# A four-layer image kernel on one core: convolutions whose operands alternate between a sample and a quarter image per 32 partitions, evictions on 128 partitions, and frames normalised once

## The chip, the cores and the metric

The kernel runs on one core of one Trainium2 chip. The metric is the device time of one execution in microseconds (us); lower is better. A run is quoted as the median of several executions. The engines are named as the profile names them: PE (matrix multiply, with PEld for its weight loads), DVE (vector), ACT (scalar and activation), POOL (GpSimd) and SP (the queue that issues most DMAs).

## The reference

The input `x` has 16 samples, 32 channels and 128 x 128 points, all float32. Four layers follow one another, each of the form `x = x + layer(groupnorm(x))`, with 16 groups of 2 channels.

- Layer 0 is a recurrent network over columns (a convolution on skewed rows feeding an LSTM of 128 steps).
- Layer 1 is a 3 x 3 convolution in which a difference takes the place of the product. Every output is minus the sum of |patch - weight| over 32 channels and 9 taps, for 32 output channels, on quantised values.
- Layer 2 is a spectral layer: a Hartley transform, a mix of 32 x 32 modes, and the inverse.
- Layer 3 is a small U-shaped network, whose output multiplies its own normalised input.

Only layer 3 is changed:

```python
orig = x
y = get_operator(x)              # 5 edge filters, each normalised: 160 channels
y = maxpool2(conv3x3(y, conv1_w, conv1_b))   # 128 -> 64
y = maxpool2(conv3x3(y, conv2_w, conv2_b))   # 64 -> 32
y = maxpool2(conv3x3(y, conv3_w, conv3_b))   # 32 -> 16
y = conv3x3(y, conv4_w, conv4_b)
y = conv3x3(deconv2x2(y, deconv1_w, deconv1_b), conv5_w, conv5_b)   # -> 32
y = conv3x3(deconv2x2(y, deconv2_w, deconv2_b), conv6_w, conv6_b)   # -> 64
y = conv3x3(deconv2x2(y, deconv3_w, deconv3_b), conv7_w, conv7_b)   # -> 128
return orig * y
```

## The kernel before

**Three stages.** `stage0` runs layer 0, from 0 to some 684 us. `rest` then runs layer 1 (`Differences`) together with layers 2 and 3 (`After`), which work on groups of 4 samples: 0 to 2 beside layer 1, group 3 after it. From 5658 us on, what is left of group 2 and the whole of group 3 are drained without layer 1; this is called the tail here.

**Layer 1.** One of 32 units is half a sample (`Differences.run`, L709). For each of its 72 taps (8 blocks of 4 output channels x 9) one instruction writes relu(q - w) for 128 x 8192 points, on DVE (L758) or on ACT (L755), whichever by the planner ends first. PE sums each tap by 16 matmuls of 512 columns in two bytes per element (`sums`, L645). So 2304 taps are shared by DVE and ACT, and PE has to follow.

**The planner.** `Weave` keeps a clock for PE, DVE and ACT when the program is written. The work of groups 0 to 2 is a generator that yields PE times, waits (negative numbers, `SUMMED`) and ("done", step). `Weave.advance` (L434) takes its next step only if PE, by the plan, is free less than 3 us (`SLACK`) after the next tap is due; evictions and normalisations are put into `later` lists with a due time. When the background has nothing to do, `keep_busy` (L669) fills PE with matmuls on zeros. `keep_order` fixes each engine's order. In the tail, `drain` (L453) takes steps from group 2 ("left") and group 3 ("right") by their plan clocks; group 3 alone has two sets of four PSUM banks.

**Layer 3 for one group.** The phases are, in order:

- `back` (L1231) ends layer 2 and stores x3 to DRAM. `frames` (L1336) loads x3 in 8 chunks of 16 rows plus borders, `[128, 20, 132]`, with 128 partitions = 4 samples x 32 channels; `normalise` (L1359) applies the group norm in place on ACT (L1363) and copies border columns (L1369, L1370).
- `statistics` (L1377) makes on PE (L1404) the products from which the filters' means and variances come. From them one folded 5 x 5 kernel `wf` is built (L1531, L1533; its tables are loaded by POOL's queue, L1518).
- `conv1` (L1663) loads and normalises all chunks a second time. Each chunk takes 25 taps x 16 matmuls, a 32 x 32 tile for each of 4 samples (row group `blk`) and 4 strips of 4 rows (column group `j`): `acc[blk][32j:32j+32]` is strip j of sample blk (L1722). Two adds per bank correct the border columns (L1758), `pooled` takes the 2 x 2 maximum (L1646).
- `spread` (L1650) then adds the bias and moves the result: as a strip lies on the partitions of its column group, and the next layer wants a sample on its own 32 partitions, each bank takes four instructions of 32 partitions, on ACT (L1660) or DVE (L1657).
- `small_layers` (L1545) does conv2 to conv4 (L1569) and the two upsampled convolutions, in which deconvolution and convolution are one (`Composed.round`, L892; matmuls L903, bias edges L928); all of them use `spread`.
- `last` (L1778) does the third upsampled convolution on `y6`, and the product with the layer's input: DVE takes a bank out of PSUM (L1851), multiplies by (x3 - mean) in a second instruction (L1814), ACT adds the mean (L1824), and SP stores 4 DMAs for each of 4 units (L1830).

One fp32 matmul stands as two matmul instructions and two weight loads in the profile.

Of the kernel before, what the change touches and what calls it, by code (L numbers as in the profile page):

```python
# [19 lines left out]
M1 = 32  # L20
RND = 12582912.0
# [469 lines left out]
def rest(nc, tc, cst, sel16, bias, m1, r1, a, d, out):  # L491


    with ExitStack() as ctx:
# [16 lines left out]
        end.buffers = {"t_x": 8, "xm": 8, "xw": 4, "t_w": 6, "t_r": 8, "frames": 4, "gm": 5, "e_v": 6, "l_x": 4}  # L511
# [319 lines left out]
class Composed:  # L831
# [60 lines left out]
    def round(self, src, n, acc, pick):  # L892

        nc, t = self.nc, self.t
        for tap in range(4):
            for j in range(4):
                par, row, rows, o = pick(j)
                top, left = row + par // 2 + tap // 2, par % 2 + tap % 2  # L900
                for blk in range(4):
                    part = slice(32 * blk, 32 * blk + 32)
                    nc.tensor.matmul(  # L903
                        acc[blk][32 * j : 32 * j + 32, o : o + rows * n],
                        t[part, 4 * par + tap, :],
                        src[part, top : top + rows, left : left + n],
                        start=tap == 0,
                        stop=tap == 3,
                        skip_group_check=True,
                    )  # L910
            yield rows * n / 512 * 0.2 + 0.95
            if tap != 2:
                continue
            for j in range(4):
                par, row, rows, o = pick(j)
                pr, pc = par // 2, par % 2
                col = o + pc * (n - 1)
                parts = [(2 + pc, slice(col, (rows - 1) * n + col + 1, n), rows)]
                if row == 0 and pr == 0:
                    parts += [(0, slice(o, o + n), n), (4 + pc, slice(col, col + 1), 1)]  # L920
                if row + rows == n and pr == 1:
                    at = (rows - 1) * n
                    parts += [(1, slice(o + at, o + at + n), n), (6 + pc, slice(at + col, at + col + 1), 1)]
                for k, to, width in parts:
                    for blk in range(4):
                        part = slice(32 * blk, 32 * blk + 32)
                        b = self.bd[part]
                        nc.tensor.matmul(  # L928
                            acc[blk][32 * j : 32 * j + 32, to],
                            t[part, 16 + k, :],  # L930
                            bass.AP(b.tensor, b.offset, [list(b.ap[0]), [0, width]]),
                            start=False,
                            stop=False,
                            skip_group_check=True,
                        )
            yield 0.4
# [20 lines left out]
class After:  # L957
# [378 lines left out]
    def frames(self, g, pool):  # L1336
# [5 lines left out]
        ring = [pool.tile([128, 20, W + 4], F32, name=f"xp{i}") for i in range(self.buffers["frames"])]  # L1342
# [4 lines left out]
        chunk = lambda ch: ring[ch % len(ring)]  # L1347

# [10 lines left out]
        def normalise(ch, half, us):  # L1359
            t, lo, hi, v = parts(ch, half)  # L1360

            def step():
                nc.scalar.activation(v, v, AF.Identity, bias=self.shift3, scale=self.stats3[:, 1])  # L1363
                for edge, r, src, zero in ((lo == 0, 1, 3, 0), (hi == H, 18, 16, 19)):
                    if edge:
                        nc.gpsimd.memset(t[:, zero, :], 0.0)
                        nc.scalar.copy(t[:, r, 2 : W + 2], t[:, src, 2 : W + 2])
# [7 lines left out]
        return load, normalise, chunk  # L1375

    def statistics(self, g, pool, frames, sides, out, tables):  # L1377
# [8 lines left out]
        load, normalise, chunk = frames  # L1386
# [26 lines left out]
        for ch in range(H // 16):  # L1413
            xp = chunk(ch)
            yield ("done", ready[ch, 0])
            for l in range(2, 18):
                if l == 8:
                    yield ("done", ready[ch, 1])
                r = 16 * ch + l - 2
# [25 lines left out]
                def following(ch=ch, half=half):  # L1445
                    load((ch + ahead) % 8, half)
                    if ch + ahead < H // 16:
                        ready[ch + ahead, half] = normalise(ch + ahead, half, 18.0)

# [55 lines left out]
    def first_layers(self, g, fp, frames, y2):  # L1505
# [32 lines left out]
        with self.pool("e_y1") as y1p:  # L1538
            y1 = self.padded(y1p, 64, "y1")
# [5 lines left out]
    def small_layers(self, cp, rp, y1, y2):  # L1545
# [3 lines left out]
        if not y1:  # L1549
# [3 lines left out]
            y3, y4, y5 = (self.padded(cp, n, f"y{i}") for n, i in ((16, 3), (16, 4), (32, 5)))  # L1553
# [3 lines left out]
        def conv(src, n, name, evict):  # L1557
            rows = min(n // 4, 512 // n)
            for r in range(0, n, 4 * rows):
                acc = [self.acc() for _ in range(4)]  # L1560
                if r:
                    weave.done(self.rest_of_y1)
                for tap in range(9):
                    kh, kw = tap // 3, tap % 3
                    for j in range(4):
                        for blk in range(4):
                            part = slice(32 * blk, 32 * blk + 32)
                            at = r + rows * j + kh
                            nc.tensor.matmul(  # L1569
                                acc[blk][32 * j : 32 * j + 32, : rows * n],  # L1570
                                wc[name][part, tap, :],
                                src[part, at : at + rows, kw : kw + n],
                                start=tap == 0,
                                stop=tap == 8,
                            )
                    yield rows * n / 512 * 1.0 + 0.15
                yield SUMMED
                for blk in range(4):
                    evict(r, rows, acc[blk][:, : rows * n], blk)
                yield -2.0  # L1580

        def pool_into(dst, n, b):
            def evict(r, rows, acc, blk):
                top, half = 1 + r // 2, rows // 2
                self.spread(
                    lambda part, j: dst[part, top + half * j : top + half * j + half, 1 : 1 + n // 2],
                    self.pooled(cp, acc, rows, n),
                    blk,
                    bias[:, b : b + 1],
                    nc.vector,  # L1590
                )

            return evict

        def flat(r, rows, acc, blk):
            self.spread(
                lambda part, j: y4[part, 1 + r + rows * j : 1 + r + rows * j + rows, 1:17],
                acc.rearrange("p (r w) -> p r w", w=16),
                blk,
                bias[:, 3:4],  # L1600
                nc.vector,
            )

        def upsampled(src, n, up, dst):

            rows = min(n, 512 // n)
            for r in range(0, n, rows):
                acc = [self.acc() for _ in range(4)]
                yield from up.round(src, n, acc, lambda j: (j, r, rows, 0))
                yield SUMMED  # L1610
                for blk in range(4):
                    self.spread(
                        lambda part, j: dst[
                            part,
                            1 + 2 * r + j // 2 : 2 * (r + rows) + j // 2 : 2,
                            1 + j % 2 : 2 * n + j % 2 : 2,
                        ],
                        acc[blk][:, : rows * n].rearrange("p (r w) -> p r w", w=n),
                        blk,
                        up.bias,  # L1620
                        nc.vector if n == 16 or blk % 2 else nc.scalar,
                    )
                yield -2.0 if n == 16 else -4.5

        if y1:
            yield from conv(y1, 64, "conv2", pool_into(y2, 64, 1))
            return
        yield from conv(y2, 32, "conv3", pool_into(y3, 32, 2))
        yield from conv(y3, 16, "conv4", flat)
        yield from upsampled(y4, 16, up5, y5)  # L1630
        yield from upsampled(y5, 32, up6, y6)

# [17 lines left out]
    def spread(self, dst, src, blk, b, engine):  # L1650

        nc, weave = self.nc, self.weave
        for j in range(4):
            d, s = dst(slice(32 * blk, 32 * blk + 32), j), src[32 * j : 32 * j + 32]
            bj = b[32 * j : 32 * j + 32]
            if blk % 2 == 0 if weave.alone else engine is nc.vector:
                nc.vector.tensor_scalar(d, s, bj, None, ALU.add)  # L1657
                weave.dve += 0.3
            else:
                nc.scalar.activation(d, s, AF.Identity, bias=bj)  # L1660
                weave.act += 0.45

    def conv1(self, g, pool, frames, y1, sides, wf, b1):  # L1663

        nc, tc, cst, weave, R = self.nc, self.tc, self.cst, self.weave, 16
# [7 lines left out]
        load, normalise, chunk = frames  # L1673
        ahead = self.buffers["frames"]
        ready = {(n // 2, n % 2): normalise(n // 2, n % 2, 4.0 + 3.0 * n) for n in range(2 * ahead)}
# [8 lines left out]
        for s, n in enumerate("lr"):  # L1684
            for tap in range(11):
                for j in range(4):
                    for blk in range(4):
# [3 lines left out]
                        else:  # L1691
                            v = sides[rows, tap // 2 + 4 * j, 2 * s + tap % 2 : 2 * s + tap % 2 + 1]
# [338 lines left out]
```

## Time and profile before

| what | value |
|---|---|
| time, median of 3 runs (lowest to highest) | 6746.03 us (6745.6 to 6754.69) |
| profiled execution: its time / its span | 6751.99 us / 6750.2 us |
| busy over the span | PE 80%, DVE 84%, ACT 82%, POOL 1% |
| granted PE clock, mean | 0.913 |
| layer 1 with groups 0 to 2 | 684 to 5658 us |
| tail | 5658 to 6750 us |
| first / last conv1 matmul of group 2 and group 3 | 5597 (border columns) / 6552 us |

A line of groups reads: line, engine, operation, output <- input with shapes, count | busy us in total, mean ns of one | idle time of the engine before them, and what ended it. A line of stages gives the length, then for each engine its busy us (and instructions), the granted PE clock, the share of the DMA engines and GB/s. Line numbers are those of the kernel before.

### The profile page before, as it was taken

The page shows a single profiled execution, that of the slowest core. Times are in us where ns is not written, and L with a number is a line of the kernel's source. Part 1 is how long each engine was busy: PE and PEld are TensorE (multiplying, and loading weights), DVE is VectorE, ACT ScalarE, POOL GpSimd, SP SyncE. Part 2 cuts the span into 40 slices and gives each one's busy share as a digit, 9 for nine tenths or more (in the row PEclk, how much of TensorE's full clock was granted, in tenths as well). Part 3 has the DMA queues.
Part 4 walks back from the last instruction along what each step waited for, and adds up shares of the span by engine and source line. Part 5 has one row for each costly group of instructions (what it writes and reads, how often), then busy time and mean ns, then how long its engine had stood idle before and what let it go on. Part 6 is the DMA issues. An engine that isn't in the chain of part 4 may idle for free.

```text
span 6750.2 us, 271326 instructions
## 1 busy us (share of the span) xinstructions
PE 5402.1 (80%) x127212; PEld 2825.9 (42%) x127212; DVE 5639.1 (84%) x6966; ACT 5552.5 (82%) x3399; POOL 85.9 (1%) x83
## 2 busy tenths in 40 slices
PE   3798777788777879997877779998787788887795
PEld 3675333333343433333333433333333343454573
DVE  7898999999999999999999998899999996144223
ACT  3898999999999999999999999999999996122112
POOL 0000000000000000000000010000000000000000
PEclk9899899999989989998898989999898998987897
DMA  7553312213244432213453543221544434355304
GB/s 319 201 190 124 79 49 64 60 31 71 72 135 117 130 84 55 61 37 79 92 153 83 158 116 74 55 62 35 118 114 125 127 92 114 121 155 127 76 25 105
DMA packets 382823, 689.09 MB, mean 102 GB/s; under 512 B 69188, under 2 KB 235588, under 8 KB 370820
## 3 DMA queue, kind: packets, MB, share of 16 engines
q1 hardware_dynamic: 374228, 637.31, 34.3%
q0 software_dynamic: 7040, 33.80, 1.5%
q8 instruction: 995, 16.30, 1.0%
q14 instruction: 128, 1.05, 0.1%
q10 hardware_dynamic: 432, 0.64, 0.0%
HBM read 507.28 MB, written 164.32 MB: 99 GB/s over the span
## 4 chain that ended last, share of the span: by engine, by line
PE 21%; issue 14%; DVE 8%; ACT 6%; DMA 2%; SPq 1%; POOL 0%; DVEq 0%; ACTq 0%; POOLq 0%
PE acc L1722 8%; ACT d_act L755 5%; PE acc L645 5%; DVE d_dve L758 4%; PE acc L903 2%; PE acc L1404 1%; PE acc L1569 1%; DVE y L1657 1%; ACT xp L1363 0%; DMA mix<-in_mix_dram 0%; PE acc L928 0%; DMA v<-fold_d 0%; PE acc L1694 0%; DMA xm_d<-xm 0%; PE acc L1313 0%
## 5 line engine op out<-in xcount | busy, mean ns | idle before, releaser
L755 ACT ACTIVATE d_act<-q,neg 128x8192 f16<-128x8192 f16 (+1 forms) x626 | 4432.4, 7146 | 149.9 <-PE acc L645 127.3
L758 DVE TENSOR_SCALAR d_dve<-q,qw 128x8192 f16<-128x8192 f16 (+1 forms) x1678 | 3870.0, 2360 | 187.0 <-PE acc L645 167.5
L645 PE MATMUL acc<-d_dve,sel 128*32 128x512 f16 x26848 | 1881.1, 403 | 540.3 <-DVE d_dve L758 461.2
L645 PEld LDWEIGHTS <-sel 128*32 128x32 f16 x36864 | 1010.4, 100 | 2137.3 <-issue 1485.5
L1722 PE MATMUL acc<-xp,wf 32*32 32x512 f32 x25600 | 1012.0, 623 | 33.0 <-issue 28.3
L645 PE MATMUL acc<-d_act,sel 128*32 128x512 f16 x10016 | 728.4, 413 | 263.5 <-ACT d_act L755 257.7
L1660 ACT ACTIVATE y<-pooled,b 32x128 f32<-32x128 f32 x464 | 185.7, 400 | 497.4 <-DVE pooled L1646 491.2
L1722 PEld LDWEIGHTS acc<-xp,wf 32*32 32x32 f32 x25600 | 431.8, 105 | 387.3 <-issue 307.4
L675 PE MATMUL acc<-q,zero 128*32 128x512 f16 x6720 | 481.9, 399 | 0.0
L903 PE MATMUL acc<-y,u_conv 32*32 32x256 f32 (+1 forms) x9728 | 356.5, 485 | 95.7 <-issue 53.0
L221 PE MATMUL pg<-h,wb 64*64 64x20 f32 (+15 forms) x8192 | 344.5, 307 | 56.3 <-DVE h L249 31.9
L235 ACT ACTIVATE gt<-pg,bias 128x20 f32<-128x20 f32 (+15 forms) x1024 | 331.3, 383 | 39.8 <-PE pg L221 37.8
L221 PEld LDWEIGHTS pg<-h,wb 64*64 64x64 f32 x8192 | 254.1, 152 | 131.4 <-DVE h L249 79.0
L1363 ACT ACTIVATE xp<-xp,shift,stats 128x1280 f32<-128x1280 f32 (+1 forms) x128 | 182.5, 1432 | 124.9 <-DMA xp<-x_d 79.4
L675 PEld LDWEIGHTS <-zero 128*32 128x32 f16 x6720 | 200.2, 101 | 185.6 <-issue 38.3
L1404 PE MATMUL acc<-xp 32*64 32x204 f32 (+3 forms) x8576 | 239.6, 346 | 36.6 <-issue 35.8
L903 PEld LDWEIGHTS acc<-y,u_conv 32*32 32x32 f32 x9728 | 167.0, 113 | 220.5 <-issue 141.7
L1758 DVE TENSOR_TENSOR acc<-acc,cut 128x4 f32<-128x4 f32 x256 | 35.2, 164 | 232.5 <-PE acc L1722 230.1
L1404 PEld LDWEIGHTS acc<-xp 32*64 32x64 f32 (+1 forms) x8576 | 175.2, 136 | 111.1 <-issue 103.6
L1851 DVE TENSOR_SCALAR s<-acc,l_ms,l_one 128x512 f32<-128x512 f32 x128 | 101.1, 814 | 142.2 <-PE acc L903 142.2
L1824 ACT ACTIVATE xr<-xr,l_ms 128x1024 f32<-128x1024 f32 x64 | 69.8, 1139 | 180.0 <-DVE xr L1814 180.0
L221 PE MATMUL pg<-xn,wb 64*64 64x2 f32 (+63 forms) x4096 | 187.2, 294 | 24.1 <-issue 13.1
(218 smaller groups left out, 3833.6 us busy)
## 6 DMA issues: line engine op xcount, KB each, us to landing
xp<-x_d SPq DMA_DIRECT2D x112, 640.0 KB, 5.1
q<-q_d SPq DMA_DIRECT2D x128, 536.2 KB, 10.0
xr<-x_d SPq DMA_DIRECT2D x128, 512.0 KB, 7.0
x_in<-in_x_dram SPq DMA_DIRECT2D x16, 2048.0 KB, 14.8
xn<-in_xs_dram SPq DMA_DIRECT2D x64, 512.0 KB, 7.3
res<-in_x_dram SPq DMA_DIRECT2D x64, 512.0 KB, 8.7
x_d<-res SPq DMA_DIRECT2D x64, 512.0 KB, 4.9
xq<-x_d SPq DMA_DIRECT2D x256, 128.0 KB, 3.5
```

The lines of the kernel that those rows point to most:

```text
L221: nc.tensor.matmul(bank[c][q][64 * pair : 64 * pair + 64, :, :width], wb[half, 4 * kind + KIND[q]].rearrange("p b o -> p (b o)"), v[half], ...
L235: nc.scalar.activation(gt[:, q, :, :n], bank[c][q][:, :, :n], AF.Tanh if q == G else AF.Sigmoid, bias=bias[:, KIND[q] : KIND[q] + 1],)
L645: self.nc.tensor.matmul(acc[k][32 * j : 32 * j + 32, :], self.sel16[:, i // 9, :], d[:, row : row + 4, c : c + W], start=first, stop=last,)
L675: self.nc.tensor.matmul(acc[k][32 * j : 32 * j + 32, :], self.zero, q[:, :4, :W], start=False, stop=False)
L755: nc.scalar.activation(dst, src, AF.Relu, bias=self.neg[:, i : i + 1])
L758: nc.vector.tensor_scalar(dst, src, self.qw[:, i : i + 1], 0.0, ALU.subtract, ALU.max)
L903: nc.tensor.matmul(acc[blk][32 * j : 32 * j + 32, o : o + rows * n], t[part, 4 * par + tap, :], src[part, top : top + rows, left : left + ...
L1363: nc.scalar.activation(v, v, AF.Identity, bias=self.shift3, scale=self.stats3[:, 1])
L1404: nc.tensor.matmul(gram[blk][j : j + width, at : at + n], xp[part, l, 2 + j : 2 + j + width], xp[part, rows, j : j + width + 4], start=sta ...
L1660: nc.scalar.activation(d, s, AF.Identity, bias=bj)
L1722: nc.tensor.matmul(acc[blk][32 * j : 32 * j + 32, :], tap_of("all", tap)[rows], xp[rows, 4 * j + kh : 4 * j + kh + 4, kw : kw + W], start= ...
L1851: nc.vector.tensor_scalar(s.rearrange("p r w b -> p b r w"), acc[blk].rearrange("p (b r w) -> p b r w", b=2, w=64), istd[:, blk : blk + 1] ...
```

## The change

1. **Operands alternate.** `conv1` no longer takes 16 neighbouring rows of the image at a time but a window of 4 rows in each of its 4 quarters (loaded with borders as `[128, 4 x 8, 132]`). Column group j is then quarter j, and after 8 windows `acc[blk]` has filled, on 128 partitions = quarter x channel, sample blk. So `y1` holds a quarter image per 32 partitions with samples along the free dimension (`quartered`), and one instruction of 128 partitions evicts a bank (`evict`). The next convolution reads quarter = row group, sample = column group, which brings its output back to a sample per 32 partitions, and so on: y2 by sample, y3 by quarter, y4 by sample, y5 by quarter, y6 by sample. `neighbours` copies border rows between quarters (DVE, 6 instructions for each of y1, y3, y5).
2. **Upsampled convolutions** of 16 and 32 points take one parity at a time (64 columns) or one pair of parities per round (256 columns), where they took all four at once with 256 or 512 columns.
3. **Frames normalised once.** `statistics` stores each normalised frame with its borders to a new DRAM buffer `xn`; `conv1` loads windows from there (`again`) and does not normalise, and `last` takes its factor from there.
4. **`last`** does eviction and product in one instruction: (acc + one) x v, with v the normalised input and one = 1/istd + bias, a constant per channel and sample; ACT adds the mean as before. Stores go out as 16 DMAs per unit, in rows of 512 bytes.
5. **Small.** One add per bank for both border columns; frames' zero rows by DVE in place of POOL; group 3 has 3 frame buffers, of 32 rows, in place of 4 of 20; the descriptor scratch of POOL's DMAs is set to 4096 bytes.

```diff
-    def round(self, src, n, acc, pick):
+    def round(self, n, rows, acc, pick):
...
+                    par, o, src, _, _ = pick(part, blk, j)
+                    top, left = par // 2 + tap // 2, par % 2 + tap % 2
                     nc.tensor.matmul(
                         acc[blk][32 * j : 32 * j + 32, o : o + rows * n],
                         t[part, 4 * par + tap, :],
-                        src[part, top : top + rows, left : left + n],
+                        src[:, top : top + rows, left : left + n],
...
-        ring = [pool.tile([128, 20, W + 4], F32, name=f"xp{i}") for i in range(self.buffers["frames"])]
+        ring = [pool.tile([128, 32, W + 4], F32, name=f"xp{i}") for i in range(self.buffers["frames"])]
...
+        def store(ch, half):
+
+            top, bottom = (0 if ch == 0 else 2, 10)[half], (10, 20 if ch == H // 16 - 1 else 18)[half]
+            nc.sync.dma_start(padded(ch, top, bottom), chunk(ch)[:, top:bottom, :])
+
+        def again(ch):
+
+            t = self.d["xn"]
+            rows = bass.AP(
+                t.tensor, t.offset + g * 128 * PADDED + 4 * ch * PW, [[PADDED, 128], [32 * PW, 4], [1, 8 * PW]]
+            )
+            nc.sync.dma_start(window(ch).rearrange("p (q r) w -> p q (r w)", q=4), rows)
...
-    def spread(self, dst, src, blk, b, engine):
+    def evict(self, dst, src, b, blk, engine=None):
...
-        for j in range(4):
-            d, s = dst(slice(32 * blk, 32 * blk + 32), j), src[32 * j : 32 * j + 32]
-            bj = b[32 * j : 32 * j + 32]
...
+        if blk % 2 == 0 if weave.alone else engine is not nc.scalar:
+            nc.vector.tensor_scalar(dst, src, b, None, ALU.add)
+            weave.dve += us
+        else:
+            nc.scalar.activation(dst, src, AF.Identity, bias=b)
+            weave.act += us + 0.15
...
+    def neighbours(self, t, n, above=True, below=True):
+
+        w = t.shape[3]
+        for q in range(3):
+            a, b = t[32 * q : 32 * q + 32], t[32 * q + 32 : 32 * q + 64]
+            if above:
+                self.nc.vector.tensor_copy(b[:, :, 0, 1 : w - 1], a[:, :, n, 1 : w - 1])
+            if below:
+                self.nc.vector.tensor_copy(a[:, :, n + 1, 1 : w - 1], b[:, :, 1, 1 : w - 1])
...
-            yield ("done", ready[ch, 0])
-            yield ("done", ready[ch, 1])
...
-                            xp[rows, 4 * j + kh : 4 * j + kh + 4, kw : kw + W],
+                            xp[rows, 8 * j + kh : 8 * j + kh + 4, kw : kw + W],
...
-                for half in range(2):
-                    load(ch + ahead, half)
-                    ready[ch + ahead, half] = normalise(ch + ahead, half, 26.0 + 4.0 * half)
+                again(ch + ahead)
...
+                    self.evict(
+                        y1[:, blk, 1 + 2 * ch : 3 + 2 * ch, 1:65], out[blk], b1[:, blk : blk + 1], blk, nc.scalar
+                    )
+                if ch in (0, 7):
+                    self.neighbours(y1, 16, ch == 7, ch == 0)
...
-                for j in range(4):
-                    nc.sync.dma_start(at(self.out, unit, j), x[32 * j : 32 * j + 32])
+                for blk in range(4):
+                    for j in range(4):
+                        first = self.out.offset + (g * 4 + blk) * CHW + (32 * unit + 8 * j) * W
+                        rows = bass.AP(self.out.tensor, first, [[HW, 32], [W, 8], [1, W]])
+                        nc.sync.dma_start(rows, inner(x)[32 * j : 32 * j + 32, blk])
...
+                        nc.vector.scalar_tensor_tensor(
+                            v,
+                            acc[blk].rearrange("p (b r w) -> p r w b", b=2, w=64),
                             one[:, blk : blk + 1],
+                            v,
+                            ALU.add,
                             ALU.mult,
```

## The prediction

> **What bounds the kernel now.** I read the stages first, then the groups of layer 1's stretch, then the waits. The stages (length, then busy us of PE, PEld, DVE, ACT, POOL):
>
> ```profile
> 684.00:5658.00 4974.00, 4062.34 (x87594) 1879.88 (x87597) 4713.76 (x3973) 4802.53 (x1275) 74.50 (x56) 0.92 0.33 87
> 2440.00:3020.00 580.00, 547.39 (x12099) 205.70 (x12103) 529.48 (x339) 543.90 (x226) 0.23 (x1) 0.95 0.23 56
> 3020.00:3300.00 280.00, 220.56 (x5290) 98.19 (x5282) 257.26 (x271) 262.08 (x77) 0.00 (x0) 0.88 0.33 76
> 5658.00:6750.00 1092.00, 870.21 (x27315) 565.81 (x27306) 363.79 (x943) 236.50 (x452) 9.00 (x20) 0.87 0.40 106
> ```
>
> Beside layer 1, DVE (94.8%) and ACT (96.5%) are the bound. Of PE's 4062 us, 482 are the zero matmuls of L675, so it has room, but not everywhere: 2440 to 3020 is conv1 of group 0, where PE is 94% busy (zero matmuls: 0.6 us). 3020 to 3300 is its conv2 to `last`, with PE 79% busy and DVE crowded. In the tail DVE and ACT idle and PE works 80%.
>
> Groups between 684 and 5658 us:
>
> ```profile
> L755 ACT ACTIVATE d_act<-q,neg 128x8192 f16<-128x8192 f16 (+1 forms) x626 | 4432.4, 7146 | 149.9 <-PE acc L645 127.3 <-DMA co_c<-in_conv_dram 18.0 <-issue 3.3
> L1363 ACT ACTIVATE xp<-xp,shift,stats 128x1280 f32<-128x1280 f32 (+1 forms) x84 | 120.1, 1429 | 0.0
> L1660 ACT ACTIVATE y<-pooled,b 32x128 f32<-32x128 f32 x256 | 102.4, 400 | 15.1 <-DVE pooled L1646 11.8
> L1660 ACT ACTIVATE y<-acc,b_conv 32x512 f32<-32x512 f32 x32 | 23.7, 740 | 14.3 <-PE acc L903 13.9
> ...
> L758 DVE TENSOR_SCALAR d_dve<-q,qw 128x8192 f16<-128x8192 f16 (+1 forms) x1678 | 3870.0, 2360 | 187.0 <-PE acc L645 167.5 <-DMA co_c<-in_conv_dram 16.2
> L626 DVE SCALAR_TENSOR_TENSOR xr<-acc,sumw,xr 128x512 f32<-128x512 f32 x124 | 84.3, 742 | 4.1 <-PE acc L645 4.1
> L1851 DVE TENSOR_SCALAR s<-acc,l_ms,l_one 128x512 f32<-128x512 f32 x64 | 50.1, 804 | 0.0
> L1814 DVE SCALAR_TENSOR_TENSOR xr<-xr,l_ms,s 128x512 f32<-128x512 f32 x64 | 46.2, 742 | 0.0
> L1657 DVE TENSOR_SCALAR y<-pooled,bias 32x128 f32<-32x128 f32 x64 | 17.9, 280 | 1.3
> L1758 DVE TENSOR_TENSOR acc<-acc,cut 128x4 f32<-128x4 f32 x128 | 21.1, 165 | 2.4
> L1093 DVE COPY xm<-acc 128x128 f32<-128x128 f32 x24 | 6.7, 284 | 1.1 <-PE acc L1089 1.0
> ```
>
> A tap costs DVE 2.36 us and ACT 7.15 us. Every us that groups 0 to 2 no longer take from them becomes taps: both engines make 1/2.36 + 1/7.15 = 0.564 taps per us, so x us off DVE and y off ACT shorten the stretch by 0.752x + 0.248y, if PE follows.
>
> **What the Trainium skill says.** *TensorEngine Tiling (Array Packing)*, PSUM Bottleneck: tiling makes TensorE faster but not the emptying of PSUM. The trace agrees: 128 columns cost DVE 280 ns on 32 partitions (L1657) and 284 on 128 (L1093), so four strips in one instruction save three of four. *VectorE: DVE Perf Modes*, Why PSUM operands drop a tier: an fp32 operand in PSUM leaves one element per cycle. L1851 and L626 agree (804 and 742 ns for 512), so the merged instruction of `last` costs about one of them. *Runtime: NRT & Kernel Launch*, Instruction fetch mechanics: instructions come in blocks of 256 by a DMA queue of the engine's own, mostly hidden. The block size agrees (995 packets, 16.30 MB: 16.4 KB each), the hiding doesn't: between 6600 and 6750 us PEld idles 41.0 us before L903 for "issue".
>
> **The change, part by part.** First, layer 1's stretch.
>
> *ACT.* conv1's evictions: 256 x 400 ns become 64, -76.8. Normalisation: 84 become 48 (3 groups x 16, statistics only), 36 x (1.43 + two border copies at 0.21) and 5 rows at 0.3: -68.1. up6: 32 x 740 become 8, -17.8. Sum -163.
>
> *DVE.* `last`: L1851 and L1814, 96.3 together, become 64 x 0.76 = 48.6. The merged form with its strided read isn't in the trace; below I take 0.74 (L626), above 1.05 (L1280, a 512-column copy in a scattered order); 0.76, since its SBUF side is contiguous like L626's. -48. L1657 (39.5 with b_conv, 25.9 pooled, 9.0 conv4: 74.4) becomes 16 x 0.28 (up5) + 8 x 0.74 (up6) + 32 x 0.28 = 19.4: -55. L1758: half of 21.1, -10. New: `neighbours`, per group 6 copies each of 256, 64 and 128 elements at 0.42, 0.19 and 0.28 = 5.3 (between L1657's rows), two groups: +11; zero rows from POOL +1. Sum -101.
>
> Gain 0.752 x 101 + 0.248 x 163 = 116; since the engines are some 95.7% busy, 122. PE decides what this does to the background. In conv1 a group frees 69 us of ACT and 3 of DVE, 11 taps; PE has no room there, so at about 1 us a tap conv1 ends 11 us later. In conv2 to `last` it frees 50 us of DVE and 9 of ACT, 22 taps; there PE idles 60 us, which takes them and the 800 more matmuls of up5/up6 (below). So the background stands 2 x 11 us later, and with 18 us of its own DVE and ACT work left over (taps went at 0.447 per us from 4880 to 5610, at 0.517 before group 0 began: 13% of some 140 us) **layer 1 ends 140 us earlier**.
>
> *The tail* starts with a background that is 140 + 22 = 162 us behind: at 5496 of the old time, late in group 2's statistics. The old 5496 to 5658 held 19.3 (L1404), 9.0 (L1694) and 11.7 (L1722) us of PE for group 2, 40 together; PE is shared and 80% busy, so +50. Its building of `wf` (14 us of DVE) lies beside group 3's matmuls.
>
> up5: per group 64 matmuls of 256 columns become 256 of 64, edges 48 to 96; up6: 128 become 256, edges 64 to 96: 400 matmuls more, 800 PE instructions with as many loads. The tail issues some 29 such pairs per us (1157 in 6360 to 6400), conv4 48 per us (210 in 4.36 us): 17 to 28 us per group. Against it stand the evictions: up6's last 16 strips end 8 us after its matmuls, now 1.5; up5's and conv4's save 3. Group 3, alone then: +10. Group 2, mixed with it: +15. `last`: PE waited 25 us for L1851's banks, of which DVE's shorter list returns 8. At the end four steps at 0.81 + 0.74 become four, -3; the final 16 stores instead of 4 cost SP 12 more issues at 0.3 to 0.5 us, half hidden by ACT's 4 x 1.14: +3. So **the tail grows by 50 + 10 + 15 - 8 = 67 us**.
>
> *DMAs.* Per group 8.9 MB of stores and 17.3 MB of windows take the place of 10.2 MB of reloads: 64 MB more in all, 305 us at the 210 GB/s that loads reach. Rows of 512 bytes aren't slower: xp's loads land 640 KB in 5.1 us. The stores stand on SP behind ACT's normalisation, whose end the plan awaits before it issues them; the first windows wait for the last stores. What queues behind on SP are layer 1's q and xr loads, issued half a unit early. conv1's two-buffer ring has a whole chunk (about 70 us beside layer 1) for a 10 us load. POOL's queue loses memsets that waited for PE. For PE's fetch beside these loads I take **+12**.
>
> Sum: -140 + 67 + 12 = -61 from the profiled execution's 6751.99 (span 6750.2). The median of the runs is 6.0 lower: 6746 - 61 = **6685 us**.
>
> **Rivals.** *A, the tail absorbs more (0.17):* PE idles 222 of the tail's 1092 us; if group 2's remainder goes into these gaps, 50 + 15 shrink to 15: 6635. Against it: 6440 to 6560 is already full. *B, PE takes the gain (0.12):* in conv1 PE waits are what holds the taps (44.7 us before L758 and 29.6 before L755 in 580); if they grow by what ACT saves (some 40 us over two groups) and by 20 in the other phases, 6745. *C, the supply of PE instructions (0.14), slower:* 6617 to 6660 has the DMA engines 97% busy and PE 20.5 of 43 us; 6680 to 6720, at 37%, 28.7 of 40. So PE loses 0.24 us per us of full DMA; if all 305 us cost that, 73 in place of 12, and group 2's and 3's extra matmuls aren't hidden (2 x 27 in place of 25), it is 6685 + 61 + 29 = 6775. It decides once fetching costs 75 us more than I count. Against it: PE has room beside layer 1. *That the change doesn't do what it says:* four strips in one instruction follow from the slices in the diff; I give it nothing.
>
> **Numbers.** Likeliest case 0.57 (6650 to 6730). A measurement of this kernel can tell about 0.2% (13 us) from no change. Faster: 0.57 and 0.17, less 0.01; same: B and a little of C, 0.12; slower: 0.15. The range runs from inside A to inside C: the merged instruction at 1.05 adds 15 us, layer 1's end is good to 25, the tail to 30.
>
> **What would show it.** Right: one ACT row of 128x128 from conv1 with about 96 in the stretch, normalisations halved, one DVE row per bank in `last` near 0.76 us; layer 1 ending near 5520; group 2 in its statistics then; a tail near 1160. Wrong: waits of L755 and L758 on L645 that grow by more than 40 us; a merged row at 1 us; a tail beyond 1220; PE idle for "issue" beside the window loads.

## The result, and the profile after

The kernel after takes 6745.84 us (median of 12 runs, 6739.97 to 6760.22), the kernel before 6741.97 us beside it (12 runs, 6729.07 to 6759.82). The ratio is 1.0007, with a 95% interval of 0.9996 to 1.0018: no change that can be told, where 6685 had been forecast. The profiled execution has a span of 6743.5 us.

The stages of the kernel after, by the same columns as before (length, then busy us of PE, PEld, DVE, ACT, POOL; granted PE clock, DMA share, GB/s):

```profile
684.00:5506.00 4822.00, 3963.38 (x86316) 1834.39 (x86315) 4556.10 (x3625) 4670.72 (x920) 47.05 (x36) 0.93 0.35 94
2440.00:3020.00 580.00, 545.28 (x12492) 209.64 (x12496) 539.67 (x330) 558.17 (x113) 0.00 (x0) 0.97 0.25 66
3020.00:3300.00 280.00, 229.51 (x6162) 108.73 (x6153) 241.52 (x203) 258.09 (x52) 0.00 (x0) 0.91 0.36 81
5506.00:6744.00 1238.00, 937.86 (x31642) 581.85 (x31638) 297.98 (x821) 117.71 (x198) 12.77 (x24) 0.87 0.44 129
```

Layer 1 ends 152 us earlier, at 5506 in place of 5658, and the tail is 146 us longer: 1238 in place of 1092, of which PE is busy 68 us more and idle 78 us more. (The last matmul of `sums` ends at 5663 and 5506, so these ends are good to some 5 us.) Nearly all of the gain is returned in the tail. In the second and third lines the new layout shows as instructions: ACT issues 165 in these 860 us where it issued 303, and PE 18654 where it issued 17389.

The groups of layer 1's stretch, with the columns of before and the line numbers of the kernel after:

```profile
L757 ACT ACTIVATE d_act<-q,neg 128x8192 f16<-128x8192 f16 (+1 forms) x633 | 4478.5, 7160 | 133.1 <-PE acc L647 111.6 <-DMA co_c<-in_conv_dram 18.1 <-issue 3.0
L760 DVE TENSOR_SCALAR d_dve<-q,qw 128x8192 f16<-128x8192 f16 (+1 forms) x1671 | 3853.4, 2361 | 203.9 <-PE acc L647 184.5 <-DMA co_c<-in_conv_dram 16.2
...
L1368 ACT ACTIVATE xp<-xp,shift,stats 128x1280 f32<-128x1280 f32 (+1 forms) x38 | 54.5, 1435 | 6.5 <-DMA xp<-x_d 6.5
L1925 DVE SCALAR_TENSOR_TENSOR xr<-acc,l_one,xr 128x512 f32<-128x512 f32 x64 | 43.5, 741 | 0.0
L1707 ACT ACTIVATE y<-pooled,b 128x128 f32<-128x128 f32 x64 | 21.8, 393 | 8.1 <-DVE pooled L1695 8.0
```

The relief is there as priced: 64 evictions at 393 ns for 256 at 400, one merged instruction of 741 ns for two of 804 and 742, and 38 normalisations for 84. The taps' waits for PE hardly move (111.6 and 184.5 us, before 127.3 and 167.5).

Where did the gain go? The phase of up5 and up6 shows a part of the answer. These are the four groups' stretches from the first matmul of up5 to the last of up6, found by counting their matmuls, first in the kernel before (groups 0, 1, 2, 3), then in the kernel after:

```profile
3130.00:3174.00 44.00, 34.96 (x861) 14.49 (x854) 40.53 (x42) 36.45 (x14) 0.00 (x0) 0.84 0.08 21
4695.00:4736.00 41.00, 34.52 (x820) 14.47 (x815) 39.19 (x39) 33.55 (x13) 0.00 (x0) 0.83 0.01 3
6095.00:6143.00 48.00, 40.35 (x1481) 24.38 (x1474) 17.93 (x46) 18.91 (x32) 0.21 (x1) 0.96 0.39 103
6594.00:6617.00 23.00, 20.70 (x608) 12.32 (x608) 9.96 (x20) 10.22 (x20) 0.00 (x0) 0.73 0.01 4
```

```profile
3128.00:3191.00 63.00, 50.91 (x1845) 26.99 (x1845) 49.09 (x40) 46.85 (x10) 0.00 (x0) 0.86 0.05 13
4748.00:4812.00 64.00, 54.28 (x1940) 28.84 (x1936) 52.77 (x38) 54.24 (x11) 0.00 (x0) 0.95 0.02 4
6180.00:6248.00 68.00, 52.56 (x2309) 36.53 (x2298) 8.64 (x27) 2.97 (x6) 0.00 (x0) 0.95 0.10 36
6582.00:6623.00 41.00, 26.84 (x1408) 20.69 (x1396) 3.91 (x13) 2.58 (x6) 0.00 (x0) 0.69 0.02 4
```

Every group takes 18 to 23 us longer, beside layer 1 as well as in the tail: 236 us in place of 156, +80. The last line of each is group 3 alone, with nothing to share PE with; its 608 and 1408 instructions are those of up5 and up6 and no others.

### The profile page after: what moved, and what is told of

The parts are those of the page before. It is cut to its first block, busy times and chain, and to the rows that moved or that the text cites. A ratio compares the mean times of both kernels' runs of the same rounds, so it can differ in the third digit from the quotient of the medians.

```text
span 6743.5 us, 276622 instructions
## 1 busy us (share of the span) xinstructions
PE 5367.8 (80%) x130260; PEld 2793.2 (41%) x130260; DVE 5415.6 (80%) x6497; ACT 5302.5 (79%) x2790; POOL 62.2 (1%) x67
## 4 chain that ended last, share of the span: by engine, by line
PE 33%; issue 31%; DVE 20%; ACT 13%; DMA 2%; SPq 1%; POOL 0%; DVEq 0%; ACTq 0%; POOLq 0%
PE acc L1788 12%; DVE d_dve L760 12%; PE acc L647 9%; ACT d_act L757 9%; PE acc L905 3%; PE pg L223 3%; ACT gt L237 2%; PE acc L1594 2%; PE acc L1426 1%; DVE stat L124 1%; ACT junk L198 1%; PE acc L932 1%; ACT th L247 1%; DMA v<-fold_d 1%; PE acc L1762 1%
## 5 line engine op out<-in xcount | busy, mean ns | idle before, releaser
L757 ACT ACTIVATE d_act<-q,neg 128x8192 f16<-128x8192 f16 (+1 forms) x633 | 4478.5, 7160 | 133.1 <-PE acc L647 111.6
L760 DVE TENSOR_SCALAR d_dve<-q,qw 128x8192 f16<-128x8192 f16 (+1 forms) x1671 | 3853.4, 2361 | 203.9 <-PE acc L647 184.5
L1788 PE MATMUL acc<-xp,wf 32*32 32x512 f32 x25600 | 1032.4, 616 | 54.9 <-issue 52.4
L1788 PEld LDWEIGHTS acc<-xp,wf 32*32 32x32 f32 x25600 | 382.3, 104 | 428.5 <-issue 344.6
L1707 ACT ACTIVATE y<-pooled,b 128x128 f32<-128x128 f32 x124 | 46.0, 398 | 516.7 <-DVE pooled L1695 516.5
L905 PEld LDWEIGHTS acc<-y,u_conv 32*32 32x32 f32 x12288 | 191.3, 108 | 199.2 <-issue 149.9
L1925 DVE SCALAR_TENSOR_TENSOR xr<-acc,l_one,xr 128x512 f32<-128x512 f32 x128 | 87.1, 743 | 202.3 <-PE acc L905 202.3
L1368 ACT ACTIVATE xp<-xp,shift,stats 128x1280 f32<-128x1280 f32 (+1 forms) x64 | 91.6, 1435 | 153.5 <-DMA xp<-x_d 127.8
L1822 DVE TENSOR_TENSOR acc<-acc,cut 128x8 f32<-128x8 f32 x128 | 18.5, 166 | 189.8 <-PE acc L1788 189.7
```

The lines of the kernel that those rows point to most:

```text
L757: nc.scalar.activation(dst, src, AF.Relu, bias=self.neg[:, i : i + 1])
L760: nc.vector.tensor_scalar(dst, src, self.qw[:, i : i + 1], 0.0, ALU.subtract, ALU.max)
L905: nc.tensor.matmul(acc[blk][32 * j : 32 * j + 32, o : o + rows * n], t[part, 4 * par + tap, :], src[:, top : top + rows, left : left + n], ...
L1788: nc.tensor.matmul(acc[blk][32 * j : 32 * j + 32, :], tap_of("all", tap)[rows], xp[rows, 8 * j + kh : 8 * j + kh + 4, kw : kw + W], start= ...
L1925: nc.vector.scalar_tensor_tensor(v, acc[blk].rearrange("p (b r w) -> p r w b", b=2, w=64), one[:, blk : blk + 1], v, ALU.add, ALU.mult,)
```

## The experiments

Times are compared as ratios to the kernel before, run beside each experiment on the same chip; "against after" is the difference from 1.0007, times 6745 us, good to some 12 us.

**e1 and e2: the tail taken apart.** In both kernels (the first change leaves the plan's waits in the tail as they are, in place of 1.5 times as long):

```diff
-        w.draining, w.stretch = True, 1.5
+        w.draining, w.stretch = True, 1.0
...
-        drain(weave, end.weave)
+        drain(weave)
+        end.weave.alone = True
+        drain(end.weave)
```

e1, kernel before: 

> Kernel before, but in the tail group 2's remainder is drained first and alone, and group 3 only after it, alone (with both sets of PSUM banks from its start). Layer 1's stretch is untouched. Theory T (the gain of layer 1 was given back because group 2's remainder, with its waits, moved into the tail): the remainder alone takes about 420 us (95% of conv1 at 70 us a chunk less layer 1's share, conv2 to conv4, last), group 3 alone 850 to 950. Rival D (the new layout makes group 3 itself longer): group 3 alone is here at least 50 us shorter than in the same run of the kernel after.

e2, kernel after: 

> Kernel after with the same edit. Theory T: group 3 alone within 25 us of what it takes in the kernel before, and group 2's remainder alone 180 to 250 us longer than there, a quarter or more of that growth with PE idle. Rival D (more matmuls, 3 frame buffers, window traffic): group 3 alone longer by 50 us or more, the remainder longer by under 150 us.

One execution each: 6863.11 and 6899.09 us. Group 2's last matmuls end at 6134 in e1 and 6126 in e2, and all but a few of group 3's come after them. So group 2's remainder takes 469 us in e1 (from 5665) and 617 in e2 (from 5509), +148; group 3 takes 727 and 771, +44, of which its statistics are 31 (126 us in place of 95). Both theories missed on group 3, which grew by more than T allowed and less than D asked; the remainder's growth is at the edge of D's 150 and short of T's 180. Undecided.

**e3: the removed work put back.** In `conv1`, `evict` and `last`, for groups 0 to 2:

```diff
+            for _ in range(more):
+                nc.scalar.activation(dst[:32], src[:32], AF.Identity, bias=b[:32])
...
+                v = t[:, 10 * half : 10 * half + 10, 2 : W + 2]
+                nc.scalar.activation(v, v, AF.Identity)
...
+                            nc.vector.tensor_scalar(acc[blk], acc[blk], 0.0, None, ALU.add)
```

> Kernel after with the engine time that the change took off DVE and ACT put back for groups 0 to 2: each eviction followed by three repeats on 32 partitions, each window passed through ACT in place (two instructions of 1280 elements and border copies, awaited as before), one more DVE pass over each bank in last. Results keep their values. Theory T: layer 1 ends about 130 us later than after (5620 to 5660), the tail is shorter by nearly as much, and the time is within 30 us of after (6720 to 6775). Rival E (layer 1's gain counts in full and something else of the change costs 120): 6745 + 120 = about 6865.

6852.48 us, ratio 1.0152 (1.0138 to 1.0166), 98 us more than after. Its stages:

```profile
684.00:5713.00 5029.00, 4038.54 (x88130) 1882.87 (x88129) 4708.84 (x3973) 4796.53 (x1272) 55.59 (x45) 0.92 0.35 94
5713.00:6854.00 1141.00, 901.28 (x29890) 573.81 (x29890) 304.60 (x833) 148.82 (x302) 7.94 (x15) 0.86 0.41 121
```

Layer 1 ends 207 us later than in after, and the tail is only 97 us shorter. My theory T, that an earlier end of layer 1 is worth nothing, falls: about half of it counts. The time is within 13 us of rival E, by which something else in the change costs about as much as the relief brings.

**e4: the relief alone.** Kernel before with:

```diff
-        for j in range(4):
-            d, s = dst(slice(32 * blk, 32 * blk + 32), j), src[32 * j : 32 * j + 32]
-            bj = b[32 * j : 32 * j + 32]
+        for j in range(1):
+            d, s, bj = dst(slice(0, 128), blk), src, b
...
-                    ready[ch + ahead, half] = normalise(ch + ahead, half, 26.0 + 4.0 * half)
...
-                        nc.vector.tensor_scalar(
+                        nc.vector.scalar_tensor_tensor(
```

> Kernel before in its old layout, with only DVE and ACT relieved: one eviction of 128 partitions per bank in place of four of 32 (so the layout of the data is wrong), conv1's second normalisation left out, one add per bank for the border columns, last's two DVE instructions merged into one (product with the unnormalised frame). No more matmuls, no stores of frames, no windows, 4 frame buffers. Theory T: layer 1 ends near 5520, the background stands as late as in after, the tail grows by over 90 us, and the time is 6700 to 6750. Rival E (the gain was eaten by matmuls, traffic or frame buffers, which are absent here): 6746 - 120 = about 6625.

6655.32 us, ratio 0.9865 (0.9852 to 0.9879): 91 us faster than before, 96 faster than after.

```profile
684.00:5456.00 4772.00, 3922.16 (x84766) 1813.76 (x84765) 4550.90 (x3577) 4641.68 (x915) 53.30 (x41) 0.93 0.34 87
5456.00:6658.00 1202.00, 930.14 (x30150) 576.71 (x30134) 285.65 (x779) 117.78 (x196) 13.36 (x27) 0.85 0.41 109
```

The relief alone ends layer 1 202 us earlier and makes the tail 110 us longer. Against it the kernel after loses 50 us in layer 1 and 36 in the tail: about 96 us by the ratios is what the rest of the change costs. So E holds in what it looks for, though not in its "in full": over half of layer 1's 202 us comes back in the tail.

**e5b, e6b, e7b: which part is it?** e5b, in `Composed.round`:

```diff
+        taps = {16: (0,), 32: (0, 3), 64: (0, 1, 2, 3)}[n]
...
-            for j in range(4):
+            for j in range(4 if tap in taps else 0):
...
-            yield rows * n / 512 * 0.2 + 0.95 if rows * n > 64 else 0.3
+            if tap in taps:
+              yield rows * n / 512 * 0.2 + 0.95 if rows * n > 64 else 0.3
```

The last lines take the PE time of the steps that are cut out of the planner's plan as well, 12 us per group.

> Kernel after with up5's rounds cut to 1 of 4 taps and up6's to 2 of 4 (so their sums are incomplete): 64 and 128 matmul pairs per group as in the kernel before, bias edges unchanged. The earlier runs leave about 88 us that the change costs besides what it relieves (51 in layer 1, 35 in the tail). Theory M (the 320 more matmul pairs per group): 14 us per group in layer 1 and 15 to 25 per group in the tail come back, 50 to 80 us: 6665 to 6695. Rivals S (stores of the frames and window loads) and R (ring of three frames): 10 to 25 us at most, 6720 to 6735.

6644.83 us, ratio 0.9860 (0.9844 to 0.9876), 99 us less than after. More than expected: the matmuls that remain also have fewer columns than in the kernel before (up5's 64 for 256, up6's 256 for 512). The four stretches of up5 and up6 take 32, 38, 40 and 23 us, less than before had. Layer 1 ends at 5499, 7 us earlier; nearly all is in the tail, which a background further on reaches shorter.

e6b, in `store`, `again` and `last`:

```diff
-            nc.sync.dma_start(padded(ch, top, bottom), chunk(ch)[:, top:bottom, :])
+            return
...
-            t = self.d["xn"]
+            t = self.d["x3"]
```

> Kernel after without the stores of the normalised frames (35.7 MB of writes, 64 DMAs); windows and last read as many bytes from x3 in place of xn (so wrong values are convolved). Theory S: statistics in layer 1 give back 7 taps, 14 us, and in the tail the 20 us that group 3's statistics grew, and PE waits less at the tail's start: 6690 to 6715. Theory M: within 15 us of after (6730 to 6755).

6732.53 us, ratio 0.9986 (0.9980 to 0.9993), 14 us less than after. S as the main cause falls; the stores have a small price.

e7b, `"frames": 3` to `"frames": 4` for group 3: 

> Kernel after with four frame buffers for group 3 in place of three (windows too are then four ahead). Theory R (three buffers make group 3's statistics 20 us longer): 15 to 25 us less than after, 6720 to 6730. Theories M and S: within 8 us of after.

6753.86 us, ratio 1.0015 (1.0008 to 1.0022), 5 us more than after. R falls.

**e9: the suspected cost doubled.** In `Composed.round`, for up6:

```diff
+                    for part_of in range(2 if n == 32 else 1):
+                        few = rows // 2 if n == 32 else rows
+                        at, row = o + part_of * few * n, top + part_of * few
```

> Kernel after with each matmul of up6 split into two of half the columns (4 rows in place of 8): 256 more pairs per group, the same columns in all, the same results. In the traces up5 and up6 take 64 to 68 us per group in after against 40 to 48 before (44 against 24 for group 3 alone): some 20 us for 400 more pairs, 0.05 us a pair. If the number of instructions sets this (theory M), 256 pairs cost 13 us per group, all of it reaching the end as a later background: 4 x 13 = 51, so 6797 (6775 to 6815). If the columns or the waits between rounds set it: within 10 us of after (6735 to 6755).

6804.35 us, ratio 1.0082 (1.0069 to 1.0095): 51 us more than after, as worked out. Up5 and up6 of group 3 alone are now:

```profile
6633.00:6688.00 55.00, 37.00 (x1920) 32.95 (x1920) 4.14 (x15) 2.88 (x8) 0.00 (x0) 0.78 0.02 4
```

55 us where after had 41, with the DMA engines 2% busy; the other groups took 74, 77 and 84. The columns are the same, so it is the instructions: 256 pairs, 512 matmul instructions with their weight loads, in each of four groups cost 51 us, 0.025 us an instruction (0.019 to 0.031 by the intervals). One thing differs from the kernel after beside the number: the two halves follow each other on the same 32 x 32 tile. No run separates this.

**e13 and e14: beside layer 1, or in the tail?** e5b's cut under `if self.g in (0, 1)`, and then `(2, 3)`.

e13: 

> Kernel after with e5b's cut (up5 1 of 4 taps, up6 2 of 4, sums incomplete) in groups 0 and 1 alone, whose up5 and up6 lie beside layer 1. As the prediction had it (PE's gaps take these matmuls beside layer 1): within 10 us of after, 6735 to 6755. If they cost their full time there too, as fewer taps and a later background: two groups of four, half of the 100 us of e5b: 6685 to 6710.

e14: 

> The same cut in groups 2 and 3 alone, whose up5 and up6 lie in the tail. As the prediction had it (25 us for these two groups, and the cut leaves out some columns as well): 6710 to 6725, and e5b's 100 us would have to be found in these two groups. Full time for every group: 40 to 55 us less than after, 6690 to 6705, so that e13 and e14 together make up e5b.

e13: 6680.47 us, ratio 0.9921 (0.9905 to 0.9937), 58 us less than after. e14: 6695.62 us, ratio 0.9944 (0.9931 to 0.9956), 42 less. The two make up e5b's 99. The larger part comes from groups 0 and 1, which the prediction had given nothing. Up5 and up6 of the two groups that are cut, first groups 0 and 1 in e13, then groups 2 and 3 in e14:

```profile
3130.00:3159.00 29.00, 25.90 (x1047) 14.43 (x1040) 28.68 (x29) 23.81 (x7) 0.00 (x0) 0.94 0.06 14
4706.00:4743.00 37.00, 25.90 (x956) 13.73 (x948) 32.23 (x36) 26.12 (x6) 0.00 (x0) 0.86 0.43 98
```

```profile
6180.00:6223.00 43.00, 37.54 (x1522) 26.61 (x1505) 6.79 (x23) 2.16 (x4) 0.00 (x0) 0.88 0.03 7
6556.00:6578.00 22.00, 14.73 (x768) 11.34 (x768) 3.98 (x13) 2.71 (x7) 0.00 (x0) 0.68 0.02 4
```

The time follows these stretches. Over all four groups they sum to 236 us in after, 133 in e5b, 178 in e13, 194 in e14 and 290 in e9: -103, -58, -42 and +54 us, and the time moved by -99, -58, -42 and +51. What up5 and up6 take is paid in full in whichever group it lies. As groups 0 and 1 of e13 take 19 us less than in the kernel before, its 58 us are more than the added matmuls of these two groups cost. Stages of e13:

```profile
684.00:5498.00 4814.00, 3956.68 (x86119) 1842.58 (x86123) 4558.40 (x3640) 4675.77 (x940) 46.75 (x36) 0.93 0.35 96
5498.00:6678.00 1180.00, 919.68 (x30651) 584.90 (x30635) 293.59 (x811) 103.95 (x173) 12.75 (x24) 0.86 0.43 129
```

Though it cuts only work that lies beside layer 1, layer 1's end moves by 8 us and the tail by 58: group 2's first matmuls of layer 2 come at 4982, as in the kernel before (4983), in place of 5060. So here a delay beside layer 1 is carried by the background and paid in the tail. That depends on the plan, from which the cut took these steps too: in e9, whose plan is that of after, layer 1 ends 26 us later (5532) and the tail is 39 us longer (1277), so that the groups beside layer 1 are paid at layer 1's end.

**e10: a version without that cost.** up5 and up6 back to one parity per column group and y5 by sample; all else as after:

```diff
+                yield from up.round(
+                    n, rows, acc, lambda part, blk, j: (j, 0, src[part, r:], r == 0, r + rows == n)
+                )
...
+                    for j in range(4):
+                        part = slice(32 * blk, 32 * blk + 32)
```

> Kernel after, but up5 and up6 as in the kernel before: one parity per column group (64 and 128 matmul pairs per group), y4 to y6 by sample, four evictions of 32 partitions per bank for these two. Theory M: the 88 us of the extra matmuls come back, less what the evictions cost again (per group some 19 us of DVE and 18 of ACT, so 18 us of layer 1 for each of two groups, half of which the tail returns, and 8 us for each of the two groups in the tail: 20 to 50): 6680 to 6710, faster than both kernels. If e5b's gain came from leaving out columns: 6735 or more.

6681.02 us, ratio 0.9904 (0.9889 to 0.9919): 69 us less than after and 1.0% faster than before, so it beats both kernels. Up5 and up6 take 44, 44, 39 and 22 us again; layer 1 ends at 5536 and the tail is 1126 in the profiled execution, the fastest of four.

**e8b, e11, e12: the planner's SLACK at 5**, `SLACK, CLOCK = 5.0, 1.0`, in after, e10 and before.

e8b: 

> Kernel after with the planner's SLACK at 5 in place of 3: the background gets PE more readily, layer 1's taps wait more. Theory T in its weaker form (about half of what layer 1's end moves comes back in the tail): layer 1 ends 0 to 40 us later, the tail gives back half or more, total within 15 us of after. If the background's place at layer 1's end is what counts, 20 to 40 us less than after.

e11: 

> The kernel of e10 with the planner's SLACK at 5. Were the two independent: 15 to 20 us less than e10 (6660 to 6695). If SLACK gains only because the background is late in after: equal to e10 within 8 us.

e12: 

> Control: kernel before with SLACK at 5. If SLACK's gain has nothing to do with the change: 6720 to 6735. If it pays only where the background is late at layer 1's end: within 8 us of before, 6737 to 6753.

e8b: 6726.42 us, ratio 0.9973 (0.9966 to 0.9981), 23 less than after; layer 1 ends at 5755, 249 later, and the tail is 261 shorter. e12: 6755.62 us, ratio 1.0011 (1.0003 to 1.0019), 7 more than before; end 297 later, tail 287 shorter. e11: 6730.29 us, ratio 0.9970 (0.9959 to 0.9981), 45 more than e10; end 259 later, tail only 193 shorter. So layer 1's end moves by 250 us and more, far beyond the 40 expected, in two of the three runs against the tail almost one for one. That e8b gains because its background stood late would fit e12, which has no gain, but it is not shown: e11 fits neither of its expectations, and why it loses stays open.

## Why the prediction was wrong, point by point

The predicted -61 consists of three sums. The matmuls of up5 and up6: two groups of the tail at 22 us each (the middle of "17 to 28 us"), 44, and nothing for the two beside layer 1. The DMAs: +12. All the rest is relief: -140 + 50 - 8, and the 19 us by which evictions set off the 44 to the 25 of the text: -117. Measured:

| part | predicted | measured |
|---|---|---|
| more matmuls, groups 0 and 1 (beside layer 1) | 0 | +42 (stretches, 19 + 23); e13's cut, which goes further, gives 58 |
| more matmuls, groups 2 and 3 (tail) | +44 | +38 (stretches, 20 + 18), 42 by e14's cut |
| stores and windows | +12 | +14 (e6b, stores alone) |
| relief of DVE and ACT, in its net | -117 | -91 (e4) |
| sum | -61 | +3; the two kernels differ by +5 (-3 to +12) |

**The step that failed** is the cover beside layer 1: "there PE idles 60 us, which takes them and the 800 more matmuls of up5/up6". The price of these instructions, 17 to 28 us per group, was right (18 to 23 measured); it was due in all four groups, and the two beside layer 1 had been given nothing. As I read it, PE's idle time beside layer 1 is spread among the waits of taps and evictions, whereas up5 and up6 are links of one chain: they last as long in PE's order as they have instructions, and what follows starts later. e13 shows this paid in the tail, e9 at layer 1's end.

**The relief** came out 26 us too large, and its halves were further off: -140 predicted in layer 1 and -202 measured (e4), +23 in the tail and +110 measured. As I read it, a shorter layer 1 leaves more of the background behind, which takes more DVE and ACT work out of layer 1 and more waits into the tail. That layer 1 of the kernel after ended where predicted (-152 for -140) was two errors against each other: 62 us more relief, and 50 us for what the rest of the change costs there.

**The background's lag**, 22 us predicted, was 77 at group 2's start (5060 for 4983); e4, without the matmuls, has 50. Group 2 stood early in its statistics when layer 1 ended, as a result, and not late in them.

**The tail**, +67 predicted, grew by 146. Its PE work (+68) is near the 65 counted (40 of group 2, 25 of up5 and up6); what is missing is PE's idle time, +78. The stage lines put 50 of it down to the relief: PE idles 222 us in the tail of the kernel before, 272 in that of e4, which has no added matmuls, stores or windows, and 300 in that of after. Much lies at the start, where group 2's statistics meet group 3's first steps: of the 80 us from 5500 on PE works 40, and e4 has 46 from 5456 on where the kernel before has 73 from 5654 on. In after ACT waits 52 of these 80 us for group 2's frames to land, and PE 25 for DVE's first steps of group 3. As I read it, layer 1 had covered these waits; no run isolates them.

**Prices:** evictions (393 ns), the merged instruction (741 ns for 0.76 us) and the normalisations were right, and no wait of the taps took the gain (rival B). **Rival A** fails: gaps did not take group 2's remainder. **Rival C** named instructions as the way to a loss, but for the groups of the tail and beside full DMAs; up5 and up6 ran slowly with DMA shares of 0.02 to 0.10. Its price was also misread: 0.24 is what PE loses between DMA shares of 37% and 97%, so that the lines give 0.40 us per us of full DMA, 122 us for 305 in place of 73. And that the "issue" time in the prediction is the fetch of instructions, no run here shows.

Open: whether group 3's statistics (+31 us in e2) suffer from the stores alone, and what sets the 0.025 us.

## What to carry to other kernels

A layout that saves evictions can be paid for in matmul instructions, as here, if each then covers fewer columns: count those instructions, at a price from a stretch where PE works alone, and in every group, whether or not another stage "covers" it. Here idle time in a stage did not hide added work, since that work was a link of the chain which the next stage waits for. Where two streams share engines under a planner, judge a change by the end of both together, since the end of one can be traded against the other.

## What was not expected of the hardware

A matmul instruction of up6 costs the same time whether it has 256 columns or 128. These are the two stretches of up6 in group 3, in the kernel after (512 instructions of 256 columns and 192 of bias edges) and in e9 (1024 of 128 columns and the same edges):

```profile
6602.00:6623.00 21.00, 16.30 (x704) 11.40 (x700) 2.87 (x10) 1.58 (x3) 0.00 (x0) 0.87 0.02 4
```

```profile
6652.00:6688.00 36.00, 26.48 (x1216) 23.72 (x1216) 3.45 (x12) 2.15 (x5) 0.00 (x0) 0.92 0.02 4
```

Both come to 0.030 us an instruction, waits included. The Trainium skill, *TensorE: Matmul & The Clock Gate*, section "Wait — 56ns, not 53.3ns?", states a floor of about 25 ns from start to start, however small the matmul. e9's mean of 0.025 us is near it, but the traces do not show such a floor: conv4's 48 instructions per us, quoted in the prediction, are 21 ns each, and in e9's group 3 half of the neighbouring starts in up6 lie 17 ns apart or less.

A part of the time is idle time that the profile calls issue. PE's waits in group 3's up5 and up6, before and then after (us in total, times, longest):

```profile
PE acc L903 <- ACT y L1660: 3.4, 2, 2.1
```

```profile
PE acc L905 <- issue: 9.3, 6, 2.2
PE acc L932 <- issue: 4.1, 3, 1.9
```

Before, PE waits only for evictions. After, it waits 13 of 41 us for nothing that the profile shows, in stops of up to 2.2 us, while the DMA engines are 2% busy. In e9 such stops take 17 of 55 us, so that of the 14 us which e9 adds here only 4 are stops and 10 are busy time of PE. That the supply of instructions makes these stops is not shown by any run here.
